# Transposes of the first four key chunks in one group in the scores' PSUM banks, and products' banks of their own from the beginning

## The chip, the cores and the metric

The kernel runs on one core of one Trainium2 chip. The metric is the device time of one execution in microseconds (us); the time before is 2101.18 us, the median of 3 runs (2100.68 to 2103.62). The profile is one further execution, recorded by the hardware profiler. The engines are named as the profile names them: PE is TensorE, DVE is VectorE, ACT is ScalarE, POOL is GpSimd and SP is SyncE, which only issues DMAs here. A step's transfers between SBUF and HBM are DMAs; PSUM is the memory of 8 banks per partition into which TensorE writes.

## The reference, cut to what matters

Two cross-attention layers follow each other on `x` (8 batches, 100 queries, 640 channels; 20 heads of 32 channels). The context has 722 tokens of 1024 channels: 77 of text, then 645 image tokens. Everything is in float32.

```python
# layer 0
q = split(hidden @ Wq.T)
out_text = softmax(q @ k_text * scale) @ v_text      # k, v: text @ Wk.T, text @ Wv.T
out_ip   = softmax(q @ k_ip * scale) @ v_ip          # k, v: ip @ Wk_ip.T, ip @ Wv_ip.T
x = (out_text + out_ip) @ Wo.T + bo + x
# layer 1: the same with its own weights, and
text_probs = softmax(q_all @ k_text_all * scale)     # over all channels, not by head
sem = ((text_probs @ text) @ ip.T) * scale
ip_probs = softmax(q @ k_ip * scale + 0.5 * sem) * mask
out = (text_out + ip_probs @ v_ip) @ Wout + bout + x
```

In front of the attention, the keys and values of the image tokens have to be made in each layer for each batch: 645 x 1024 by 1024 x 640, twice. This is most of the arithmetic.

## The kernel before

**Stages.** The prologue (to about 207 us) makes the queries of layer 0 and the text keys and values of both layers. Then follow the keys and values of the first pair of batches (to about 396 us), and then 80 attention steps. A step is numbered n = 5u + p: u counts (layer, batch) from 0 to 15, p the five groups of four heads; steps 0 to 39 are layer 0, 40 to 79 layer 1. A step lasts 11 to 29 us, because it also holds a share of the projections of later batches.

**A step's pieces.** `scores(u, p, 0)` (L849, tile `sc`) writes the scores of four heads on keys 0 to 511 into one tile of four PSUM banks, one head a bank. The softmax reads them there. In layer 0, VectorE takes the maximum (L855) and ScalarE makes four exponentials out of the banks (L866), so the banks are free after the last exponential. In layer 1, VectorE adds `sem` in four passes from the banks to SBUF (L862), and ScalarE's exponentials read SBUF, so the banks are free after the last pass. `scores(u, p, 1)` writes keys 512 to 721 into the same four banks: the pool `ps_sc` has one buffer. After it, VectorE and ScalarE finish the softmax (L872 to L893; L889 and L890 scale the probabilities). The probabilities are needed with keys on partitions, so one step later `transposes(u, c, j)` (L905, tile `pspt`) turns chunk j of 128 keys, four transposes of 100 columns to a chunk, six chunks; each goes to a bank of the pool `ps_pt` and is copied to the SBUF tile `pt` by VectorE (L912; chunks 0, 1, 3, 4) or ScalarE (L910; chunks 2, 5). `values` (L927, tile `pv`) multiplies `pt` by the values.

**PSUM.** Of the eight banks, four belong to `ps_sc`, two to `ps_pt` and two to `ps_pj`. The pool `ps_pt` also serves `values`, the output pieces (`pso`, L774, added to the residual by L779), query pieces (`psq`, L793, copied by L797) and layer 1's semantic products (`psm`). `ps_pj` serves the projections' products. In the prologue all eight banks are one pool, `ps_first`, and the three others are opened when it is closed.

**Order.** TensorE's order is written out by hand (`manual_schedule` for PE only); the other engines' orders follow from a scheduler. Between the pieces of a step, `between(n, a, b, small)` lays out the projections' products whose due time lies before n + b. Due times come from `production` and `spread`, which share the products of each pair of batches over ten steps, less where a step has other small work (output and query pieces, semantic products). One `seven` is a matrix product in seven half-size products (tiles `psv_a` to `psv_e` or `psk_a` to `psk_e`), whose results ScalarE (L172, L181) and VectorE (L177, L198, L203) add up in SBUF; plain products are `psk`, `psv` of L503 and L608 (copied by L509 and L610). A step has the order: first scores; products to 0.4; transposes of chunks 0, 1 of the step before; products to 0.6; chunks 2, 3; second scores directly behind; products to 0.8; chunks 4, 5; products to 1.0; values of the step before.

**End of the prologue.** Text values of layer 1 are made in two halves of rows, `text_v_blocks` (tile `vt`, L328; stored by POOL, L336). Between the halves stand `sums_of("k")`, weight sums on VectorE and POOL, and `left_v(1)` (tile `vl`, stored by L361), the last five context rows' values. Directly after it, the first pair's products begin: `psk` (L503), `psk_a`, `psk_b` (L536).

## Time and profile before

| what | us |
|---|---|
| median of 3 runs | 2101.18 |
| the profiled execution's own time | 2102.57 |
| its span | 2100.8 |
| TensorE busy | 2069.5 |
| VectorE, ScalarE, POOL busy | 941.5, 863.6, 332.6 |
| transposes (L905), busy sum | 212.6 |
| copies of transposes on VectorE (L912), ScalarE (L910) | 176.2, 78.1 |

In a line of the costliest groups, the line number and engine come first, then the operation, output and inputs, shapes (partitions x elements) and the count; then the busy sum in us and the mean of one in ns; then the idle time of the engine just before such instructions, and what ended most of it. In the timeline, a line begins with its start and its length in us; matmuls in a row with the same tile are one line, and brackets give the idle time before it and its releaser. TensorE's matmuls overlap, so their durations add up to more than the time they take; how far apart they start says more.

### The profile page before, as it was taken

Reading aid. Unit: us, or ns where it says so; the run is one execution under the profiler, and the core shown is the slowest. Engines: PE = TensorE matmul, PEld = TensorE weight load, DVE = VectorE, ACT = ScalarE, POOL = GpSimd, SP = SyncE. Lnnn points to the kernel's source line nnn. Section 1 sums busy time; section 2 is a strip of 40 time slices with the busy share of each in tenths; the row PEclk is TensorE's granted clock in tenths of the full one; section 3 lists DMA queues with packets and bytes.
Section 4 is the critical chain, followed back from the end, with each engine's and each line's share of the span. In section 5 each row is a group of like instructions: output and inputs, shape, how many; then the busy total and the mean of one; then the engine's idle time right before and its main releaser. Section 6 shows DMA issues by size and latency. Waiting matters only on the chain.

```text
span 2100.8 us, 40948 instructions
## 1 busy us (share of the span) xinstructions
PE 2069.5 (99%) x16370; PEld 1635.0 (78%) x16370; DVE 941.5 (45%) x2420; ACT 863.6 (41%) x2865; POOL 332.6 (16%) x378
## 2 busy tenths in 40 slices
PE   8999999999999999999999999999999999999999
PEld 8676787777787777787788877887878778777888
DVE  1211221345544554444454545445455454555554
ACT  1001000244433544344444544445444455676665
POOL 3313221111111111111150110111111110101110
PEclk9999999999999999999999999999999999999999
DMA  9344232323424443352544443353344345434320
GB/s 343 113 133 152 91 95 77 113 74 87 111 80 131 124 113 92 95 160 80 153 130 127 131 106 81 112 146 97 82 116 132 94 122 153 141 101 118 112 83 7
DMA packets 272493, 241.96 MB, mean 115 GB/s; under 512 B 42798, under 2 KB 241890, under 8 KB 272302
## 3 DMA queue, kind: packets, MB, share of 16 engines
q1 hardware_dynamic: 253182, 171.97, 30.0%
q0 software_dynamic: 19120, 67.37, 9.7%
q8 instruction: 129, 2.11, 0.4%
q14 instruction: 62, 0.51, 0.1%
HBM read 171.68 MB, written 67.61 MB: 114 GB/s over the span
## 4 chain that ended last, share of the span: by engine, by line
PE 95%; DVE 2%; ACT 1%; DMA 1%; issue 1%; SPq 0%; DVEq 0%; ACTq 0%
PE psv_a L528 8%; PE psv_d L528 8%; PE pspt L905 8%; PE psk_d L536 6%; PE sc L849 6%; PE psk_a L536 6%; PE psk L503 5%; PE pv L927 4%; PE psv L608 4%; PE psv_e L528 4%; PE psk L608 4%; PE psv_c L528 4%; PE psv_b L528 3%; PE psk_b L536 3%; PE psk_e L536 3%; PE psk_c L536 3%
## 5 line engine op out<-in xcount | busy, mean ns | idle before, releaser
L912 DVE COPY pt<-pspt 128x400 f32<-128x400 f32 x320 | 176.2, 569 | 191.3 <-PE pspt L905 184.2
L866 ACT ACTIVATE p<-p,st 100x512 f32<-100x512 f32 (+1 forms) x320 | 176.4, 553 | 134.6 <-DVE st L862 134.5
L866 ACT ACTIVATE p<-sc,st 100x512 f32<-100x512 f32 (+1 forms) x320 | 165.0, 528 | 142.7 <-DVE st L855 142.5
L905 PE MATMUL pspt<-ident,p 100*128 100x100 f32 (+1 forms) x1920 | 212.6, 250 | 10.3 <-DVE res L779 4.9
L905 PEld LDWEIGHTS pspt<-ident,p 100*128 100x128 f32 (+1 forms) x1920 | 187.7, 138 | 44.0 <-DVE res L779 8.5
L889 ACT ACTIVATE p<-p,st 100x512 f32<-100x512 f32 x320 | 204.8, 711 | 37.9 <-DVE st L885 37.5
L528 PE MATMUL psv_a<-wv,x 128*128 128x397 f32 (+1 forms) x560 | 185.5, 473 | 2.6 <-ACT vo L172 2.6
L910 ACT COPY pt<-pspt 128x400 f32<-128x400 f32 (+1 forms) x160 | 78.1, 488 | 253.9 <-PE pspt L905 253.1
L528 PE MATMUL psv_d<-wv,s 128*128 128x320 f32 (+1 forms) x560 | 174.7, 455 | 0.0
L528 PEld LDWEIGHTS psv_a<-wv,x 128*128 128x128 f32 x560 | 103.2, 190 | 67.1 <-issue 9.4
L552 POOL DMA_DIRECT2D v_d<-vo x70 | 39.5, 564 | 725.1 <-DVE gst L520 389.8
L862 DVE CUSTOM_DVE_ANT_0 p<-sc,sem 100x512 f32<-100x512 f32 (+1 forms) x320 | 138.8, 490 | 28.5 <-PE sc L849 28.5
L528 PEld LDWEIGHTS psv_d<-wv,s 128*128 128x128 f32 x560 | 103.9, 190 | 55.7 <-issue 5.8
L536 PEld LDWEIGHTS psk_a<-x,wk 128*128 128x128 f32 x1120 | 132.3, 192 | 12.8 <-issue 9.4
L536 PE MATMUL psk_d<-s,wk 128*128 128x128 f32 (+1 forms) x1120 | 140.0, 278 | 0.4 <-ACT ko L181 0.4
L536 PE MATMUL psk_a<-x,wk 128*128 128x128 f32 (+1 forms) x1120 | 139.2, 277 | 0.0
L849 PE MATMUL sc<-k,q 32*100 32x210 f32 (+1 forms) x1280 | 138.6, 502 | 0.3 <-ACT p L874 0.3
L536 PEld LDWEIGHTS psk_d<-s,wk 128*128 128x128 f32 x1120 | 131.2, 192 | 9.1 <-issue 3.3
L855 DVE TENSOR_REDUCE st<-sc 100x4 f32<-100x2048 f32 x80 | 120.1, 1501 | 30.4 <-PE sc L849 30.3
L503 PE MATMUL psk<-x,wk 128*128 128x256 f32 (+1 forms) x560 | 131.6, 383 | 0.7 <-DVE vt L203 0.7
L564 POOL DMA_DIRECT2D k_d<-ko x70 | 58.1, 829 | 463.2 <-DVE ko L198 427.2
L503 PEld LDWEIGHTS psk<-x,wk 128*128 128x128 f32 x560 | 102.3, 189 | 23.6 <-issue 8.5
(180 smaller groups left out, 3302.3 us busy)
## 6 DMA issues: line engine op xcount, KB each, us to landing
x<-ip_t SPq DMA_DIRECT2D x56, 512.0 KB
k<-k_d SPq DMA_DIRECT2D x78, 322.5 KB
v<-v_d SPq DMA_DIRECT2D x78, 320.0 KB
v_d<-vo POOLq DMA_DIRECT2D x70, 320.0 KB, 2.6
k_d<-ko POOLq DMA_DIRECT2D x56, 320.0 KB, 6.9
o<-wo SPq DMA_DIRECT2D x40, 320.0 KB
x<-ip_t SPq DMA_DIRECT2D x16, 532.0 KB
q<-wq SPq DMA_DIRECT2D x20, 320.0 KB
```

Of the source, the lines that this page charges most:

```text
L503: nc.tensor.matmul(ps[:, : 2 * n], lhsT=W["k", 4][:, k, :], rhs=xs[j][:, :, k, :n], start=(k == 0), stop=(k == NCC - 1),)
L528: nc.tensor.matmul(ps[:, :m], lhsT=sums[which][:, k, :P], rhs=w[:, k, :], start=(k == 0 and not go_on), stop=(k == HK - 1), skip_group_che ...
L536: nc.tensor.matmul(ps[:, r * n : (r + 1) * n], lhsT=W["k", WHICH[which]][:, k, r * P : (r + 1) * P], rhs=sums[which][:, k, :], start=(r == ...
L608: nc.tensor.matmul(ps[:m, :n], lhsT=lhs(k), rhs=rhs(k), start=(k == 0), stop=(k == NCC - 1))
L849: nc.tensor.matmul(sc[:S, i, : k1 - k0], lhsT=qs_[u][rows, c, :], rhs=ks[u, c][rows, k0:k1], start=True, stop=True)
L855: nc.vector.tensor_reduce(st[:, part, :], sc[:S, :, :n], AX.X, ALU.max, negate=True)
L862: nc.vector.tensor_tensor_reduce(out=img, in0=sc[:S, i, :n], in1=sems[u][:, k0 : k0 + n], scale=-1.0, scalar=3.0e38, op0=ALU.add, op1=ALU. ...
L866: nc.scalar.activation(p[:, i, k0 : k0 + n], img, AF.Exp, bias=st[:, part, i : i + 1], scale=sign, accum_out=st[:, 3 + part, i : i + 1],)
L889: nc.scalar.activation(p[:, i, :KA], p[:, i, :KA], AF.Copy, scale=mul[:, 0, i : i + 1])
L905: nc.tensor.transpose(ps[:rows, i * S : (i + 1) * S], pr[u, c][:, i, j * P : j * P + rows], ident[:S, :S])
L912: nc.vector.tensor_copy(dst, src)
L927: nc.tensor.matmul(ps[32 * i : 32 * i + 32, :S], lhsT=lhs, rhs=pt[:rows, j, i * S : (i + 1) * S], start=(j == 0), stop=(j == 5),)
```

## The change

The first four chunks of a step's transposes, sixteen instructions, are now issued together (`first_transposes`) into one tile of `ps_sc`, the scores' four banks, one chunk a bank. Three copies take them out: VectorE chunks 0 and 1 in one instruction of 128x800, ScalarE chunk 2, VectorE chunk 3. The group stands where chunks 0 and 1 stood; the chunks 2 and 3 in front of the second scores are gone from there, so that only products lie between the group and the second scores. Chunks 4 and 5 stay in `ps_pt`. The fractions 0.4, 0.6, 0.8 become 0.42, 0.64, 0.82. In the last step's tail the same grouping is used.

The pool `ps_pj` of the products is opened at the beginning instead of after the prologue, and the prologue's pool has six banks instead of eight. The two halves of layer 1's text values are made one after the other, and `left_v(1)` comes last.

```diff
@@ -150,10 +150,11 @@
 
 
 
+    ps_pj = ctx.enter_context(tc.tile_pool(name="ps_pj", bufs=2, space=PSUM))
+    pj = []
+
     def product_ps(name):
         return pj[0].tile([P, 512], F32, tag="pj", name=name)
-
-    pj = []
 
     def seven(name, product, area, beside=None):
 
@@ -219,7 +220,7 @@
     TR = TH - 2 * P
     with ExitStack() as es:
         fp = es.enter_context(tc.tile_pool(name="first", bufs=1))
-        pj.append(es.enter_context(tc.tile_pool(name="ps_first", bufs=8, space=PSUM)))
+        pj.append(es.enter_context(tc.tile_pool(name="ps_first", bufs=6, space=PSUM)))
         xt = fp.tile([P, B, NC_, S], F32, tag="x", name="xt")
         wq0 = []
         nc.sync.dma_start(xt[:, :2], x_t[:, :2])
@@ -319,8 +320,8 @@
                     t[64 * h : 64 * h + TR, :, :HC],
                 )
 
-        def text_v_blocks(l, rows=(0, 1)):
-            for r in rows:
+        def text_v_blocks(l):
+            for r in range(2):
                 t = fp.tile([P, 2, 2, HC], F32, tag="evs", name=f"vt_{l}_{r}", bufs=2)
 
                 def product(ps, which, go_on, r=r):
@@ -400,14 +401,13 @@
             left_text()
             text_v(1)
             sums_of("v")
-            text_v_blocks(1, (0,))
+            text_v_blocks(1)
             sums_of("k")
             left_v(1)
-            text_v_blocks(1, (1,))
 
     ps_sc = ctx.enter_context(tc.tile_pool(name="ps_sc", bufs=1, space=PSUM))
     ps_pt = ctx.enter_context(tc.tile_pool(name="ps_pt", bufs=2, space=PSUM))
-    pj[0] = ctx.enter_context(tc.tile_pool(name="ps_pj", bufs=2, space=PSUM))
+    pj[0] = ps_pj
     opool = ctx.enter_context(tc.tile_pool(name="made", bufs=2))
     kpool = ctx.enter_context(tc.tile_pool(name="k", bufs=2))
     vpool = ctx.enter_context(tc.tile_pool(name="v", bufs=2))
@@ -896,17 +896,29 @@
 
     pts = {}
 
-    def transposes(u, c, j):
-        if j == 0:
-            pts[u, c] = one.tile([P, 6, 4 * S], F32, tag="pt", name=f"pt_{u}_{c}")
+    def transpose_chunk(ps, u, c, j):
         rows = P if j < 5 else NTAIL
-        ps = ps_pt.tile([P, 512], F32, tag="pt", name=f"pspt_{u}_{c}_{j}")
         for i in range(4):
             nc.tensor.transpose(
                 ps[:rows, i * S : (i + 1) * S], pr[u, c][:, i, j * P : j * P + rows], ident[:S, :S]
             )
+
+    def first_transposes(u, c):
+
+        pts[u, c] = one.tile([P, 6, 4 * S], F32, tag="pt", name=f"pt_{u}_{c}")
+        ps = ps_sc.tile([P, 4, 512], F32, tag="sc", name=f"pspt_{u}_{c}")
+        for j in range(4):
+            transpose_chunk(ps[:, j], u, c, j)
+        nc.vector.tensor_copy(pts[u, c][:, 0:2, :], ps[:, 0:2, : 4 * S])
+        nc.scalar.copy(pts[u, c][:, 2, :], ps[:, 2, : 4 * S])
+        nc.vector.tensor_copy(pts[u, c][:, 3, :], ps[:, 3, : 4 * S])
+
+    def transposes(u, c, j):
+        rows = P if j < 5 else NTAIL
+        ps = ps_pt.tile([P, 512], F32, tag="pt", name=f"pspt_{u}_{c}_{j}")
+        transpose_chunk(ps, u, c, j)
         dst, src = pts[u, c][:rows, j, :], ps[:rows, : 4 * S]
-        if j % 3 == 2:
+        if j == 5:
             nc.scalar.copy(dst, src)
         else:
             nc.vector.tensor_copy(dst, src)
@@ -1079,16 +1091,12 @@
                 at = small_work(u, p)
                 loads(u, p)
                 scores(u, p, 0)
-                between(n, 0.0, 0.4, at[0])
+                between(n, 0.0, 0.42, at[0])
                 if last:
-                    transposes(*last, 0)
-                    transposes(*last, 1)
-                between(n, 0.4, 0.6, at[1])
-                if last:
-                    transposes(*last, 2)
-                    transposes(*last, 3)
+                    first_transposes(*last)
+                between(n, 0.42, 0.64, at[1])
                 scores(u, p, 1)
-                between(n, 0.6, 0.8, at[2])
+                between(n, 0.64, 0.82, at[2])
                 if u < LAST or p < 3:
                     load_v(u, p)
                 nu, np_ = (u, p + 1) if p < 4 else (u + 1, 0)
@@ -1097,15 +1105,16 @@
                 if last:
                     transposes(*last, 4)
                     transposes(*last, 5)
-                between(n, 0.8, 1.0, at[3])
+                between(n, 0.82, 1.0, at[3])
                 if last:
                     values(*last)
                 last = (u, p)
                 if n == NC_ * NU - 2:
                     last_out_weights()
         last_out_begin()
-        for j in range(6):
-            transposes(*last, j)
+        first_transposes(*last)
+        transposes(*last, 4)
+        transposes(*last, 5)
         values(*last)
         last_out_end()
 
```

## The prediction

> **What bounds the kernel now.** I began with the page's span, busy shares and the chain that ended last, then the costliest groups.

> ```profile
> span 2100.8 us, 40948 instructions
> PE 2069.5 (99%) x16370; PEld 1635.0 (78%) x16370; DVE 941.5 (45%) x2420; ACT 863.6 (41%) x2865; POOL 332.6 (16%) x378
> ...
> PE 95%; DVE 2%; ACT 1%; DMA 1%; issue 1%; SPq 0%; DVEq 0%; ACTq 0%
> ...
> L912 DVE COPY pt<-pspt 128x400 f32<-128x400 f32 x320 | 176.2, 569 | 191.3 <-PE pspt L905 184.2
> ...
> L905 PE MATMUL pspt<-ident,p 100*128 100x100 f32 (+1 forms) x1920 | 212.6, 250 | 10.3 <-DVE res L779 4.9
> ```

> TensorE sets the end. It is idle for 31.3 us (2100.8 - 2069.5), 5.6 of them at the start, so removing waits can gain little, and whatever makes TensorE wait is paid in full. The copies of transposes (569 ns on DVE) hold nothing up: DVE is 45% busy.

> Next, how closely TensorE's instructions follow each other, from start to start in the timeline: a transpose 86 ns, a matmul 216 ns with 256 columns, 269 with 320, 332 with 397. A product is 8 of these: 1.73, 2.15 or 2.66 us. Against them I read when the scores' banks come free: the short step 13 of layer 0 (TensorE, then ScalarE), then step 59 of layer 1 (TensorE, then VectorE).

> ```profile
> 697.54 1.12 PE L849 MATMUL sc<-k,q 32*100 32x512 f32 x8
> 698.59 2.00 PE L503 MATMUL psk<-x,wk 128*128 128x256 f32 x8
> 700.43 0.85 PE L905 MATMUL pspt<-ident,p 100*128 100x100 f32 x8
> 701.11 2.86 PE L528 MATMUL psv_a<-wv,x 128*128 128x397 f32 x8
> 703.81 0.85 PE L905 MATMUL pspt<-ident,p 100*128 100x100 f32 x8
> 704.59 0.61 PE L849 MATMUL sc<-k,q 32*100 32x210 f32 x8
> ...
> 703.63 0.21 ACT L866 ACTIVATION_READ_ACCUMULATOR p<-sc,st 100x1 f32 x1
> ...
> 1757.48 1.12 PE L849 MATMUL sc<-k,q 32*100 32x512 f32 x8
> ...
> 1762.20 0.87 PE L905 MATMUL pspt<-ident,p 100*128 100x100 f32 x8
> 1762.90 1.92 PE L608 MATMUL psk<-x,wk 128*128 128x256 f32 x8
> ...
> 1761.11 0.08 DVE L862 DVE_READ_ACCUMULATOR2_ANT st<- 100x1 f32 x1
> ```

> From the start of the first scores, their four banks are read for 6.2 to 6.3 us in layer 0, where four exponentials on ScalarE read them after VectorE's maximum (697.54 to 703.84), and for 3.71 us in layer 1, where VectorE alone reads them (1757.48 to 1761.19). In step 13 the transposes start at 2.88 us, in other banks. That is the fact on which the change turns.

> [...]

> **The change, part by part.** The order of the changed kernel's instructions is known; I price each step of it with the pitches above.

> Nothing leaves or joins TensorE's work: 24 transposes in a step before and after. The second scores' first matmul starts 93 ns later behind transposes, and as much later behind a wide product, so parting the two costs and gains 0.

> Gains. (1) Chunks 0 to 3 no longer wait for the two ps_pt buffers, which output pieces (L774), query pieces and values share. Lateness over the pitch, summed over steps: 2.84 us at chunk 1, 0.11 at 2, 4.64 at 3; 7.6 together. Chunk 5's waits (9.5 us), waits on products' copies and waits for output weights stay. (2) Products' banks are open from the beginning, and text v's stores leave earlier.

> ```profile
> 207.61 3.70 PE L503 MATMUL psk<-x,wk 128*128 128x256 f32 x16 [0.68 <-DVE vt L203]
> ...
> 208.01 0.55 POOL L336 DMA_DIRECT2D vt_d<-vt  x1 [1.85 <-DMA wv<-text_t]
> ...
> 214.38 0.37 ACT L509 COPY ko<-psk 128x256 f32<-128x256 f32 x1 [15.60 <-DVE wvt L131]
> ...
> 214.81 2.05 PE L536 MATMUL psk_b<-s,wkt 128*128 128x128 f32 x16 [1.72 <-ACT ko L509]
> ```

> The first wait is for the prologue's pool (0.84 us over the pitch). The second (1.88) is for L509's copy, held by the landing of the text-v store issued at 208.01, at 213.70. With row 1 moved ahead of left_v, that store goes about 4.5 us earlier; the last are now left_v's two, of 51 KB, which landed 1.9 us after issue where they stood at 192.4. I count on 206.8 for the first product, 212.0 for psk_b and about 211.5 for the copy: both waits gone, 2.7 us. On POOL's queue the moved stores now stand before L124's subtraction (0.85 us) and left_v's; L133, next there, waits for a load until 214.5. The key sums that trade places with row 1 are done on VectorE and POOL ahead of all these stores, many us before their first product. If the copy is still late, up to 1.9 of it returns. Six prologue banks for eight: with five tiles in a seven-product group of some 14 us and copies near 0.5 us, I take 0. Sum of gains: 10.3 us.

> Losses. (3) The sixteen transposes now need the scores' banks. In steps 13, 23 and 33 they stand 2.88 us after the first scores and are allowed at 6.36: 3 x 3.48 = 10.4 us. In layer 1 they stand before 3.77 us in nine steps (52, 60, 62, 65, 66, 70, 72, 75, 77): 0.84 + 1.01 + 0.47 + 0.58 + 0.47 + 0.95 + 0.90 + 0.96 + 0.81 = 7.0 us. All other steps have them at 4.4 us or later in layer 1, 7.5 or later in layer 0: hidden by products.

> (4) The second scores wait for the group's last copy. The built order has one signal after all sixteen transposes, then VectorE's copy of 128x800, then ScalarE's waiting for VectorE's, then VectorE's third waiting for ScalarE's: a chain. From the first transpose: 15 x 0.086 + 0.249 + 0.037 (signal to VectorE) = 1.576; copy 0.99; 0.035; ScalarE 0.492; 0.032; VectorE 0.574; 0.055 to TensorE: 3.76 us. The signal times are medians of the trace. The 800-wide copy is not in it: 0.57 plus 400 elements at 1.05 ns, the slope between the maximum's 100x532 (0.71 us) and 100x2048 (2.29). [...] Sixteen transposes and one 256-column product take 1.38 + 1.73, with 0.09 into the scores 3.2: 0.5 late in thirteen late steps (44, 59, 61, 64, 67, 69 to 72, 74, 75, 77, 78), 6.9 us. With one 320-column product 3.6: 0.15 late in eight (33, 39, 55, 60, 62, 63, 65, 66), 1.2. Elsewhere 4.0 to 6.7 us lie between. Sum 8.1. A chain of 3.60 gives 5, one of 4.1 gives 15.5. While VectorE waits for ScalarE, products' copies behind it slip by 0.56 us; two banks and a product of 1.7 us or more cover that, else up to 0.3 a step.

> (5) Later second scores shift the last softmax of the step: in steps 10, 20 and 33 the copies of chunks 4 and 5 stand behind L890's multiplication, and values follow soon; 0 to 1.15 each, I take 1 together. In the tail, values come 3.9 instead of 3.6 us after the first transpose: 0.3.

> Losses: 10.4 + 7.0 + 8.1 + 1.3 = 26.8. Net +16.5. The profiled execution took 2102.57, 1.8 about its span of 2100.8; 2117.3 + 1.8 = 2119.1. The median shown, 2101.18, lies 1.4 below it: 2117.7 us.

> **Rivals.** (A) Faster, no new wait decides: if the transposes do not wait for the first scores' readers, or products stand before them after all, 17.4 falls away, and with a chain of at most 3.2 us, 8.1 too; 2101.2 - 10.3 + 1.3 = 2092. It decides once losses (3) and (4) together stay under 9. For it: TensorE's pauses in the trace are short and a planner fills. Against: step 13's order has only one product in front, and the banks' readers end at 6.2 us in every step of layer 0.
> (B) The chain is longer: ScalarE's copy stands behind four exponentials in layer 1 (they end 4.85 us after the first scores in step 59) or VectorE's pair holds products' copies. At 4.1 us plus 0.3 in the short steps: 2117.7 + 7.4 + 3 = 2128. Against: even in the shortest steps ScalarE's copy is due at 6.4.
> (C) Parting transposes and scores does save the 93 ns, in 79 steps 7.3 us: 2110. One product-to-scores pair in the trace, 204 ns against 111, speaks against it.
> (D) The hand-over gains nothing: +2.7, 2120, inside the range.

> **Numbers.** My account, D's end included, has 0.55, C 0.12, B 0.15, A and partial forms of it 0.18. Within 0.2% (4.2 us, about what this measurement can tell from no change) needs some 12 us of error in my sum: 0.07. Faster by over 0.2%, from A: 0.14. Slower 0.79. The range runs from C with a shorter chain (2110 - 4) to B, 2106 to 2128; the likeliest case alone gives 2113 to 2124.

> **What would show it.** After: idle of 3.5 us before pspt in steps 13, 23, 33, ended by ACT L866, and of 0.5 to 1 us ended by DVE L862 in the nine; idle before sc in the thirteen, ended by the VectorE copy of chunk 3, 8 us in all; waits of pspt on res (L779) only at chunk 5; no pause at psk and psk_b near 207 and 212; a copy of 128x800 near 0.99 us. Wrong if sc or pspt show no such idle, if the chain differs from 3.76 us by 0.3, or if TensorE's busy time itself falls.

## The result, and where the time went

The changed kernel takes 2123.73 us (median of 4 runs, 2122.96 to 2125.89), the kernel before 2101.38 on the same chip: a ratio of 1.0104, 95% interval 1.0089 to 1.0119. By the medians it is slower by 22.4 us; forecast were 16.5, with a range to 2128. Here are the lines of its page that answer to those shown of before: span and busy shares, and the groups of the transposes and of the 800-wide copy.

```profile
span 2122.5 us, 40938 instructions
PE 2073.4 (98%) x16370; PEld 1628.0 (77%) x16370; DVE 933.1 (44%) x2340; ACT 864.1 (41%) x2865; POOL 332.5 (16%) x378
...
L902 PE MATMUL pspt<-ident,p 100*128 100x100 f32 (+1 forms) x1920 | 197.0, 252 | 23.4 <-ACT p L866 9.9
...
L912 DVE COPY pt<-pspt 128x800 f32<-128x800 f32 x80 | 79.3, 992 | 182.0 <-PE pspt L902 175.0
```

TensorE is idle for 49.1 us (2122.5 - 2073.4) instead of 31.3, and the idle time in front of the transposes has gone from 10.3 to 23.4 us. TensorE's busy time has risen by 3.9 us as well, with the same 16370 matmuls: some of them have become slower. The 800-wide copy takes 0.992 us, as estimated.

The waits of TensorE by releaser (us in all, times, the longest) name the new ones.

```profile
PE pspt L902 <- ACT p L866: 9.9, 3, 3.3
PE pspt L902 <- DVE st L862: 6.0, 9, 0.9
...
PE sc L849 <- DVE pt L914: 5.4, 12, 0.5
...
PE pspt L902 <- DVE res L779: 3.3, 6, 1.3
```

Three waits of 3.3 us for layer 0's exponentials, nine of up to 0.9 for layer 1's reads, and the second scores waiting for the group's last copy: the three losses that were forecast, at the places that were forecast. In the timeline, the two steps that stand for them are step 13 and step 70 (TensorE first, then the three copies of step 70).

```profile
692.38 1.12 PE L849 MATMUL sc<-k,q 32*100 32x512 f32 x8
...
698.73 2.80 PE L902 MATMUL pspt<-ident,p 100*128 100x100 f32 x16 [3.31 <-ACT p L866]
701.33 3.35 PE L528 MATMUL psv_a<-wv,x 128*128 128x397 f32 x8
704.61 0.61 PE L849 MATMUL sc<-k,q 32*100 32x210 f32 x8
...
1955.59 1.56 PE L902 MATMUL pspt<-ident,p 100*128 100x100 f32 x16 [0.87 <-DVE st L862]
1956.99 1.97 PE L608 MATMUL psv<-wvl,x 128*128 128x128 f32 x16
1959.42 0.61 PE L849 MATMUL sc<-k,q 32*100 32x210 f32 x8 [0.46 <-DVE pt L914]
...
1957.19 0.99 DVE L912 COPY pt<-pspt 128x800 f32<-128x800 f32 x1 [1.75 <-PE pspt L902]
1958.27 0.49 ACT L913 COPY pt<-pspt 128x400 f32<-128x400 f32 x1 [1.55 <-DVE pt L912]
1958.80 0.57 DVE L914 COPY pt<-pspt 128x400 f32<-128x400 f32 x1 [0.61 <-ACT pt L913]
```

Step 70 shows the chain whole: 1955.59 to 1959.42 is 3.83 us, against 3.76 forecast. Step 13 shows what was not forecast: after the pause, sixteen transposes take from 698.73 to 701.33, 2.60 us, where step 70 has 1.40; the product behind them takes 3.28 instead of 2.7. The windows view has the granted clock (PEclk) there; of a line, the first numbers are the stretch and its length, then the busy times of PE, PEld (TensorE's weight loads), DVE, ACT and POOL, each with its count of instructions, the clock, and the DMAs' share and GB/s.

```profile
690.00:698.70 8.70, 5.43 (x70) 3.48 (x69) 3.10 (x3) 3.16 (x9) 1.85 (x3) 1.00 1.07 264
698.70:701.00 2.30, 2.27 (x15) 2.27 (x16) 0.00 (x0) 0.00 (x0) 0.00 (x0) 0.55 0.30 91
701.00:704.60 3.60, 3.60 (x12) 1.99 (x10) 1.57 (x2) 0.49 (x1) 0.00 (x0) 0.82 0.00 0
704.60:708.00 3.40, 3.40 (x19) 2.27 (x19) 1.37 (x4) 2.04 (x10) 0.00 (x0) 1.00 0.41 109
```

At the hand-over from the prologue, both waits are gone:

```profile
205.40 3.72 PE L503 MATMUL psk<-x,wk 128*128 128x256 f32 x16
...
210.74 1.95 PE L536 MATMUL psk_b<-s,wkt 128*128 128x128 f32 x16
```

The account of the two traces, step by step (a step is the time between the first scores of one and of the next; `psgl` is the tile of the `left_text` products in the prologue, and `psk_a` to `psk_e` are those of the first pair):

| where | change, us |
|---|---|
| query phase at the start | -1.1 |
| hand-over: from psgl to the second psk_a, 55.95 to 52.92 | -3.0 |
| steps 13, 23, 33: 16.65, 16.65, 15.62 to 21.83, 21.86, 22.37 | +17.1 |
| steps 11, 12, 21, 22, 31, 32, 41, 42, 51 (0.3 to 0.6 each) | -4.1 |
| the other steps, nearly all of it from 44 on | +12.8 |
| tail | -0.3 |
| sum, to TensorE's last instruction | +21.4 |

The first row is no part of the change: the ten traces of this study have 35.7 to 37.0 us there, whatever the kernel. In these two traces its length goes with the moment at which TensorE's pace doubles, where the records of its granted clock begin, too: the phase's first matmuls follow each other by 0.333 us and then by 0.169, from 11.7 us after the start in the trace of before and from 9.4 in that of the changed kernel.

### The profile page after: what moved, and what is told of

Same layout as the page of the kernel before. It is cut to its first block, busy times and chain, and to the rows that moved or that the text cites. A ratio compares the mean times of both kernels' runs of the same rounds, so it can differ in the third digit from the quotient of the medians.

```text
span 2122.5 us, 40938 instructions
## 1 busy us (share of the span) xinstructions
PE 2073.4 (98%) x16370; PEld 1628.0 (77%) x16370; DVE 933.1 (44%) x2340; ACT 864.1 (41%) x2865; POOL 332.5 (16%) x378
## 5 line engine op out<-in xcount | busy, mean ns | idle before, releaser
L866 ACT ACTIVATE p<-p,st 100x512 f32<-100x512 f32 (+1 forms) x320 | 176.4, 553 | 178.2 <-DVE st L862 178.2
L866 ACT ACTIVATE p<-sc,st 100x512 f32<-100x512 f32 (+1 forms) x320 | 165.0, 528 | 193.3 <-DVE st L855 193.1
L902 PE MATMUL pspt<-ident,p 100*128 100x100 f32 (+1 forms) x1920 | 197.0, 252 | 23.4 <-ACT p L866 9.9
L902 PEld LDWEIGHTS pspt<-ident,p 100*128 100x128 f32 (+1 forms) x1920 | 180.9, 139 | 48.3 <-ACT p L866 17.2
L528 PE MATMUL psv_a<-wv,x 128*128 128x397 f32 (+1 forms) x560 | 189.0, 480 | 2.6 <-ACT vo L173 2.6
L528 PE MATMUL psv_d<-wv,s 128*128 128x320 f32 (+1 forms) x560 | 174.6, 454 | 0.0
L862 DVE CUSTOM_DVE_ANT_0 p<-sc,sem 100x512 f32<-100x512 f32 (+1 forms) x320 | 138.8, 490 | 56.9 <-PE sc L849 55.3
L912 DVE COPY pt<-pspt 128x800 f32<-128x800 f32 x80 | 79.3, 992 | 182.0 <-PE pspt L902 175.0
L528 PEld LDWEIGHTS psv_a<-wv,x 128*128 128x128 f32 x560 | 105.8, 194 | 69.1 <-issue 12.5
L528 PEld LDWEIGHTS psv_d<-wv,s 128*128 128x128 f32 x560 | 103.5, 190 | 55.8 <-issue 7.7
L849 PE MATMUL sc<-k,q 32*100 32x210 f32 (+1 forms) x1280 | 138.5, 502 | 6.3 <-DVE pt L914 5.4
L913 ACT COPY pt<-pspt 128x400 f32<-128x400 f32 x80 | 39.4, 492 | 254.8 <-DVE pt L912 254.8
L536 PEld LDWEIGHTS psk_a<-x,wk 128*128 128x128 f32 x1120 | 132.1, 191 | 12.2 <-issue 9.4
L536 PE MATMUL psk_d<-s,wk 128*128 128x128 f32 (+1 forms) x1120 | 140.3, 278 | 0.8 <-ACT ko L182 0.8
L536 PE MATMUL psk_a<-x,wk 128*128 128x128 f32 (+1 forms) x1120 | 139.1, 277 | 0.0
L536 PEld LDWEIGHTS psk_d<-s,wk 128*128 128x128 f32 x1120 | 131.0, 191 | 9.6 <-DVE hs L943 3.1
L503 PE MATMUL psk<-x,wk 128*128 128x256 f32 (+1 forms) x560 | 133.2, 383 | 0.0
L503 PEld LDWEIGHTS psk<-x,wk 128*128 128x128 f32 x560 | 101.5, 189 | 23.2 <-issue 9.4
```

The source lines that it names most:

```text
L503: nc.tensor.matmul(ps[:, : 2 * n], lhsT=W["k", 4][:, k, :], rhs=xs[j][:, :, k, :n], start=(k == 0), stop=(k == NCC - 1),)
L528: nc.tensor.matmul(ps[:, :m], lhsT=sums[which][:, k, :P], rhs=w[:, k, :], start=(k == 0 and not go_on), stop=(k == HK - 1), skip_group_che ...
L536: nc.tensor.matmul(ps[:, r * n : (r + 1) * n], lhsT=W["k", WHICH[which]][:, k, r * P : (r + 1) * P], rhs=sums[which][:, k, :], start=(r == ...
L849: nc.tensor.matmul(sc[:S, i, : k1 - k0], lhsT=qs_[u][rows, c, :], rhs=ks[u, c][rows, k0:k1], start=True, stop=True)
L862: nc.vector.tensor_tensor_reduce(out=img, in0=sc[:S, i, :n], in1=sems[u][:, k0 : k0 + n], scale=-1.0, scalar=3.0e38, op0=ALU.add, op1=ALU. ...
L866: nc.scalar.activation(p[:, i, k0 : k0 + n], img, AF.Exp, bias=st[:, part, i : i + 1], scale=sign, accum_out=st[:, 3 + part, i : i + 1],)
```

## Experiments

All ratios are to runs of the kernel before on the same chip; 0.001 is 2.1 us.

### The prologue's part alone, and half of it

`prologue_alone` is the kernel before with the prologue's part of the change; `pools_alone` leaves the text values in the old order.

```diff
+    ps_pj = ctx.enter_context(tc.tile_pool(name="ps_pj", bufs=2, space=PSUM))
-        ... name="ps_first", bufs=8
+        ... name="ps_first", bufs=6
-            text_v_blocks(1, (0,))           # in prologue_alone only
+            text_v_blocks(1)
             sums_of("k")
             left_v(1)
-            text_v_blocks(1, (1,))
```

> The kernel before with only the prologue's part of the change: products' banks open from the beginning, six prologue banks, both halves of text values ahead of left_v. Account: the two waits at the hand-over (psk, psk_b) go and nothing else moves: 2.9 us less than before, near 2098.5, no idle before psk or psk_b. Rival, the hand-over is hidden anyway or the stores land late elsewhere: 2101.4. If it is near 2098.5, the grouped transposes alone cost about 25 us.

> The kernel before with only the banks' part of the prologue's change (products' banks apart, six prologue banks), text values in the old order. Account: psk starts 0.84 us earlier, but psk_b still waits for L509's copy, which waits for the landing of the last text-v store; the store stands where it stood, so the wait grows by 0.84 and nothing is gained: ratio 1.000. Rival that the copy was late because of the pool and not of the store: the whole 2.9 us, 0.9986.

Measured: `prologue_alone` 0.998 (0.9974 to 0.9987), 2.7 to 5.5 us less; its trace has 53.28 us from psgl to the second psk_a, 2.7 less than before. `pools_alone` 1.0007 (0.9999 to 1.0016), and 56.05 us in that stretch, against 55.95. Its timeline:

```profile
205.78 3.62 PE L504 MATMUL psk<-x,wk 128*128 128x256 f32 x16
...
213.13 0.37 ACT L510 COPY ko<-psk 128x256 f32<-128x256 f32 x1 [15.34 <-DMA vt_d<-vt]
...
213.56 2.58 PE L537 MATMUL psk_b<-s,wkt 128*128 128x128 f32 x16 [2.37 <-ACT ko L510]
```

The first product starts without a wait, and `psk_b` waits that much longer, 2.37 us instead of 1.72, for a copy that is itself released by the landing of the text-v store. Behind this wait TensorE's granted clock fell to 0.50, from 214.90 to 218.31; some 0.5 us of the 56.05 are due to that (an estimate: half of the 1.03 us from 214.90 to the second `psk_a`), and the other 1.1 us or so fall behind that stretch, which is most of what the run lost to the kernel before. So of the 2.7 us the banks alone bring 0.4 at most, and the rest needs the store's earlier place. What the new order would bring with the old banks, no run shows. Together with the change's ratio, the grouping alone costs 25 to 27 us.

### What the three pauses cost: fill_14, fill_7, ungroup_3

```diff
 # fill_14, fill_7 (the lines around the insertion are unchanged)
                 between(n, 0.0, 0.42, at[0])
+                if n in (13, 23, 33):
+                    fill = product_ps(f"fill_{n}")
+                    for i in range(14):        # fill_7: 7
+                        nc.tensor.matmul(fill[:, :P], lhsT=ident, rhs=ident, start=True, stop=True)
                 if last:
                     first_transposes(*last)
```

> The changed kernel, with 14 products of the identity by itself (3.1 us, result unused) laid into the pauses of steps 13, 23 and 33, so that TensorE waits for the scores' banks as long as before but is not idle. Theory that the pause of 3.3 us lowers TensorE's granted clock: the waits stay, the slow instructions behind them go, 6.7 us less than the changed kernel: 2117.0, clock 1.0 in those steps. Rival that the instructions are slow because the grouped transposes write banks that were just read, or because ScalarE and VectorE read PSUM beside them: unchanged, 2123.7.

Measured: 1.0075 (1.0063 to 1.0088), 6.1 us less than the changed kernel's 1.0104. Step 13 with its filling (the trace records the 14 products as 28 matmuls; the last line is of the windows view):

```profile
696.34 3.29 PE L1098 MATMUL fill<-ident 128*128 128x128 f32 x28
699.80 1.59 PE L902 MATMUL pspt<-ident,p 100*128 100x100 f32 x16 [0.18 <-ACT p L866]
...
699.26:701.46 2.20, 2.02 (x21) 1.82 (x20) 0.00 (x0) 0.49 (x2) 0.00 (x0) 1.00 0.27 82
```

The transposes still start 6.35 us after the first scores, but the clock stays at 1.00, and steps 13, 23 and 33 are 1.66, 1.69 and 3.01 us shorter than in the changed kernel: 6.4 us. The transposes write the same banks, just read, and are not slow (1.59 us for the sixteen, 2.80 in the changed kernel); the idle time in front makes the difference.

> As fill_14 with 7 products instead of 14, so that TensorE is idle for about 1.9 us instead of 3.3 or 0.2 in steps 13, 23 and 33. If only a pause of about 3 us or more lowers the granted clock: as fill_14, ratio 1.0075 to before, steps 13, 23, 33 at 20.2, 20.2, 19.4 us. If a pause lowers it in proportion: about half of the 6.1 us returns, ratio 1.009.

Measured: 1.0085 (1.0071 to 1.0099), between the two forecasts. The trace tells why: with 1.75 us of idle left, step 23 and step 33 kept the clock (20.18 and 19.37 us, as in fill_14), and step 13 lost it, with 0.50 granted from 700.10 to 703.51, and took 21.85 us. So neither reading holds: the pause does not act in proportion, and the 3 us of the other reading (the changed kernel had 3.31 in front of each slow stretch) are not needed. What sorts the three steps is how the pause lies to windows of 3.413 us, at whose borders the clock changes and which do not begin with the pause (worked out from the traces at the end of the section on why the prediction was right). Step 13's pause lies within one window; step 23's begins in one and ends in the next, which holds most of it:

```profile
696.69:700.10 3.41, 1.66 (x17) 1.47 (x17) 0.00 (x0) 2.56 (x8) 0.00 (x0) 1.00 0.85 291
939.04:942.45 3.41, 1.79 (x18) 1.65 (x19) 0.09 (x1) 1.56 (x6) 0.00 (x0) 1.00 0.50 169
```

TensorE is idle for 1.75 us of the first, and the window behind it is slow. It is idle for 1.62 us of the second, and for 1.43 us of step 33's window, and the windows behind these have the full clock. How the windows lie differs between the traces: the records of the clock begin 9.42 us after the start in that of the changed kernel and 11.67 in that of before, with the first matmul at 5.49 and 5.55. Of the four executions of fill_7, three have a mean granted clock of 0.999, and the fourth, with 1.000, is the shortest by 2.1 us (2117.92); the steps can be read in the profiled one alone.

```diff
 # ungroup_3, shortened: in these three steps chunks 2 and 3 and the fractions are as before, too
+                apart_ = n in (13, 23, 33)
-                if last:
-                    first_transposes(*last)
+                if last and apart_:
+                    transposes(*last, 0, 2)
+                    transposes(*last, 1, 2)
+                elif last:
+                    first_transposes(*last)
```

> The changed kernel, with the grouping undone in steps 13, 23 and 33 alone (chunks 0 to 3 in ps_pt, placed as in the kernel before). Theory that these steps pay the pauses (3 x 3.48 = 10.4) and the slow clock after them (6.7): 17.1 less than the changed kernel, 2106.6. Rival that the slow clock comes from elsewhere and stays: 2113.3.

Measured: 1.0042 (1.0028 to 1.0056), 13 us less than the changed kernel, between the two forecasts again. By steps, 13, 23 and 33 are 5.18, 5.20 and 6.75 us shorter, 17.1 in all and as long as in the kernel before, as the theory has it. But steps 28 and 29, which were left as they were, have become 1.84 and 2.31 us longer.

### Steps 28 and 29: no_sums

In step 28, small operations of the softmax on VectorE, which the expectation calls additions (L879 takes a minimum, L880 a difference, L885 a product), had become long in ungroup_3, beside POOL's weight sums for layer 1 (L131 to L134). VectorE first, then POOL:

```profile
1055.86 2.38 DVE L879 TENSOR_TENSOR st<-st 100x4 f32<-100x4 f32 x1
...
1063.10 3.56 DVE L885 SCALAR_TENSOR_TENSOR st<-st,mask_sb 100x8 f32<-100x8 f32 x1
...
1055.54 2.69 POOL L134 TENSOR_TENSOR wvt<-wv,wvt 128x1280 f32<-128x1280 f32 x1
```

```diff
 # ungroup_3 without four of POOL's sums
     def second_weights(kind):
         (load_wv if kind == "v" else load_wk)({"v": wvi, "k": wki}[kind][1])
-        weight_sums(kind, {"v": HC, "k": 2 * P}[kind], (nc.gpsimd, nc.gpsimd))
+        if kind == "v":
+            W["v", "t1"], W["v", "t2"], W["v", "t3"], W["v", "t4"] = (W["v", f"b{x}"] for x in ("12", "11", "22", "21"))
+            return
+        weight_sums(kind, 2 * P, (nc.gpsimd, nc.gpsimd))
```

> ungroup_3 with layer 1's four weight sums for values left out on POOL (unsummed weights are used, so this part of layer 1 is not computed). ungroup_3 lost 1.84 and 2.31 us in steps 28 and 29. Theory that POOL's sums there hold up VectorE's additions with two SBUF inputs (L879 took 2.38 us, L880 2.06): both back near 0.2 us, the loss gone, 4.1 us less than ungroup_3, ratio 1.0022. Rival that it is the store of keys on POOL or a late load: unchanged, 1.0042.

Measured: 1.0024 (1.0015 to 1.0033). Steps 28 and 29 are back at 21.50 and 23.92 us, the values of the kernel before, and these operations are short again:

```profile
1054.91 0.16 DVE L879 TENSOR_TENSOR st<-st 100x4 f32<-100x4 f32 x1
...
1059.52 0.75 DVE L885 SCALAR_TENSOR_TENSOR st<-st,mask_sb 100x8 f32<-100x8 f32 x1
```

POOL's first sum waits for a load of weights that is issued 1.1 us before step 28's first scores in all these kernels. It starts 4.1 us after them in fill_14, 4.8 in the changed kernel, 6.4 in ungroup_3. At 4.8 the four sums, some 11 us in a row, are over when most of these operations come; at 6.4 they are not, L879 and L880 come out 4.1 us late together, and L885 then meets the next sums on POOL, those of the token blocks and keys (L215, L131). One long operation alone costs nothing: in the kernel before, L879 takes 2.31 us and L883 1.99 in this step, and both are hidden. What makes the load land later was not settled. The 4.1 us that ungroup_3 paid go with POOL's sums; the transposes of these two steps are as in the changed kernel.

### The chain of copies: one_copy

```diff
-        nc.vector.tensor_copy(pts[u, c][:, 0:2, :], ps[:, 0:2, : 4 * S])
-        nc.scalar.copy(pts[u, c][:, 2, :], ps[:, 2, : 4 * S])
-        nc.vector.tensor_copy(pts[u, c][:, 3, :], ps[:, 3, : 4 * S])
+        nc.vector.tensor_copy(pts[u, c][:, 0:4, :], ps[:, :, : 4 * S])
```

> The changed kernel, with the group's three copies made one VectorE copy of 128x1600. Theory that the second scores of the late steps wait for the chain of three copies: the time from the first transpose to the scores goes from 3.76 to 1.58 + 1.83 + 0.06 = 3.46 us, so 18 waits shrink by 0.3 or vanish, about 4.6 us less: 2119. Rival that these waits are set by VectorE's other work: no gain, 2123.7, or up to 2126 as VectorE is held for 1.83 us in one piece.

Measured: 1.0105 (1.0091 to 1.0119), no gain in the whole. In the waits of TensorE, the one for the group's last copy has gone from 5.4 us in 12 waits to this:

```profile
PE sc L849 <- DVE pt L912: 1.2, 6, 0.2
```

By steps, each late step that waited is 0.16 to 0.33 us shorter (44, 59, 60, 62 to 67, 69, 70, 72, 74, 75, 77, 78); with the few others from 39 on it is 4.6 us, what the theory had. Steps 28 and 29 are 1.32 and 2.33 us longer, with the same long operations (L885 at 3.58 us) and POOL's first sum at 5.9 us; that takes back 3.65. So the waits hang on the length of the chain; the total alone would have hidden it.

### Grouping only where it gains: best_14

```diff
 # best_14, shortened: where apart_ holds, as in ungroup_3
+                apart_ = n not in {11, 12, 21, 22, 31, 32, 41, 42, 51, 61, 63, 71, 73, 76}
```

> The prologue's part of the change, and the grouping only in the fourteen steps that gained by it in the changed kernel's trace (11, 12, 21, 22, 31, 32, 41, 42, 51, 61, 63, 71, 73, 76); all other steps as in the kernel before. Account: 2.9 us less from the hand-over and 7.2 us from the fourteen steps (0.40, 0.60, 0.40, 0.60, 0.39, 0.61, 0.40, 0.32, 0.39, 0.9, 0.41, 0.96, 0.25, 0.58), 10 us less than before, ratio 0.995. Rival that a step's gain comes only with delays elsewhere: prologue_alone's ratio, 0.998. If VectorE is blocked in steps 28 and 29 as in ungroup_3, 4 us less gain: 0.997.

Measured: 2091.31 us, 0.9949 (0.9937 to 0.9962), faster than both kernels. Each of the fourteen steps gained what it had gained in the changed kernel (0.26 to 0.96 us, 7.3 in all), 0.3 came from the tail, and the hand-over gave 3.0. TensorE's idle time is 26.4 us (2089.6 - 2063.2):

```profile
span 2089.6 us, 40940 instructions
PE 2063.2 (99%) x16370; PEld 1628.8 (78%) x16370; DVE 939.2 (45%) x2405; ACT 864.5 (41%) x2865; POOL 333.4 (16%) x378
```

## Why the prediction was right, point by point

- **No work leaves TensorE, and parting transposes from scores gains nothing.** Right: steps without a wait have the same length to 0.02 us in both traces, and the 93 ns of rival C would have shown in each of them.
- **Gain 1, 7.6 us of waits for the two buffers.** Right: best_14 has 7.3 us in fourteen steps (which have the changed fractions, too). Waits at chunk 5 stayed, as said.
- **Gain 2, 2.7 us at the hand-over.** Right in size (3.0 in the trace) and in cause: pools_alone shows that without the store's new place at most 0.4 comes.
- **Loss 3 in layer 1, 7.0 us.** Right: the nine steps named, 7.5 us of lateness.
- **Loss 3 in layer 0, "3 x 3.48 = 10.4 us".** This is the term that was mis-sized. The waits came where and as long as forecast (the transposes start 6.35 us after the first scores, for 6.36), but the three steps cost 17.1 us. The step priced the pause and took TensorE's pace behind it for unchanged. fill_14 shows nearly all the rest, 6.1 us by the ratios and 6.4 by the steps, to be the granted clock. That it equals the whole miss (22.4 - 16.5 = 5.9) is in part luck: smaller misses cancel (0.5 more in layer 1, 0.8 and 1.6 less in losses 4 and 5, the 1.1 of the query phase), and steps 50, 54 and 55 together are 1.1 us longer, which only in small part is a term of the sum (0.15 in step 55). Products stand at other places there, one of 1.73 us in step 54 instead of 55; what the loss hangs on was not looked into.
- **Loss 4, 8.1 us from a chain of 3.76 us.** Right: the chain is 3.83, the waits about 7.3 us beyond the usual 93 ns, in 18 of the 21 waits named; one_copy shortens them by what it takes off the chain.
- **Loss 5, 1.3 us.** Wrong by about 1.6, which is little: steps 10 and 20 did not change, and the tail gained 0.3. Step 33's share cannot be told from the clock.
- **Rivals.** A needed waits that do not decide; they do. B's end, 2128, came near the result by another mechanism than its own: its longer chain and held products are not in the trace.

The prediction had worked out the pauses at 3.48 us and left the granted clock behind them out of its sum. In the changed kernel's records it is 0.50 for 3.413, 3.413 and 6.827 us in steps 13, 23 and 33, from 698.91, 941.26 and 1176.78 us on. These moments are 71 and 69 times 3.4133 us apart, and the first is 202 times 3.4133 after 9.42, where the records begin; it lies just behind the pause of step 13. So the windows of 3.413 us are read from the traces: the stretches are one, one and two of them long, and all begin on one grid that starts at 9.42. In the trace of before, 612 of them lie between 11.67, where its records begin, and 2100.62, where the clock falls to 0.50 behind TensorE's last instruction. A clock of 0.50 for 3.41 us loses 1.7: an estimate from these records, beside 1.66 and 1.69 measured, and 3.01 for the two windows of step 33.

A window need not be idle throughout for the clock to fall behind it. Cut the ten traces along these windows: of those that end before TensorE's last instruction, eight have it idle for 1.75 us or more (1.75 in fill_7, 2.07 in pools_alone, 2.13 to 3.24 in the changed kernel and one_copy), and behind each the clock is 0.50. Of the others, with up to 1.72 us (at the hand-over of before), none has a slow window behind it, but for step 33 in the changed kernel and in one_copy, where the slow window itself, with 0.29 and 0.44 us of idle, is followed by a second one; why, stays open. So in these traces the limit lies between 1.72 and 1.75 us of idle time in one window. By this count a pause costs the clock wherever it falls only from some 3.5 us (an estimate, twice 1.75), and one of 1.75 to 3.5 us when enough of it falls into one window, as all six pauses of 3.31 us did. It is not a larger share of transposes that goes with the lost clock: of the two windows of fill_7 shown, step 23's, which kept it, holds 1.4 us of transposes and 0.4 of other matmuls, step 13's, which lost it, 0.8 and 0.9.

## What to carry to other kernels

A larger buffer borrowed from another stage brings that stage's readers with it: work out for every step when they end, and group only where they have ended and a wait for the smaller buffers goes, which here, with the prologue's part, turned 22 us of loss into 10 of gain. When TensorE is the bound, price a pause of some us by its length and by the slow stretch that may follow it (here 3.41 us at a clock of 0.50, or twice that, behind pauses of 3.31); laying matmuls into it, as in fill_14, tells the two apart. Look at the clock of several places and executions: one pause of 1.75 us cost it in step 13 of fill_7 and not in step 23, and three executions of fill_7 had a mean of 0.999, the fourth 1.000. And compare step by step, since an overlap on other engines, moved by some us, can give back in one place what was gained in another, as the 4.1 us of steps 28 and 29 in ungroup_3.
